# Row sums and sums of squares as accumulated outputs in the first three groups of an adaLN layer (one Trainium2 core)

## The chip, the cores and the metric

The kernel runs on one core of a Trainium2 chip. The time is device microseconds (us) of one execution. Engines: PE is the matrix engine, DVE the vector engine, ACT the scalar engine (activation functions), POOL the GpSimd engine, SP the engine that here only issues loads and stores. Each engine works through its own list of instructions in order; semaphores tie the lists together.

## The reference

One transformer layer on 4 x 1024 tokens of width 256, in float32. A conditioning vector c (one per batch) gives six vectors sa, ca, ga, sb, cb, gb.

```
h   = layernorm(x) * (1 + ca) + sa
q, k, v = unit(h Wq + bq), unit(h Wk + bk), unit(h Wv + bv)     # unit: f = fft; f / (|f| + 1e-8); back
s   = cumsum over tokens of bind(k, v)                          # product of spectra
x   = x + ga * unbind(s, q)                                     # product with the conjugate spectrum
h   = layernorm(x) * (1 + cb) + sb
x   = x + gb * top-2 mixture of 8 experts (swiglu, 256 -> 512 -> 256)
```

layernorm divides by sqrt(variance + 1e-5); the spectra are divided by |f| + 1e-8. These two places are the ones that matter here.

## The kernel before

**Tiles.** The 4096 tokens are 8 groups of 512 (`GT` = 4 tiles of 128 rows); two groups make a batch. A group's x is one tile of 128 x 4 x 256 (`x_tiles[g]`, three buffers), and its result rows are gathered in `row`, 128 x 4 x 266 (two buffers): 256 columns of normalized x, 8 expert weights and 2 numbers. Each group has two pairs of tiles; pairs are numbered 0 to 15 below, pair n belonging to group n // 2.

**Steps of a group.** `begin_group` (L480) takes mean and variance of each of the 512 rows (`moments`, L445: `bn_stats` L451 and `bn_aggr` L453 on DVE), the square root (ACT, L441) and its reciprocal (DVE, L442), and the shift `nmr` (L486, L487); POOL stamps token numbers into `row` (L490).

**Steps of a pair** (`pair`, L496, a generator whose pieces are interleaved with those of other pairs):

- ACT normalizes into `xn` (L505), PE transposes it (L512), ACT copies `ht` (L516);
- PE multiplies by the spectra matrix (L528), ACT copies `z` (L535) and squares it (`sq`, L537 for k and v, L541 for q);
- `magnitudes` (L545): POOL copies two end columns (L547), DVE or POOL adds real and imaginary squares (L551), ACT takes the root (L552), DVE adds EPS (L553). For k and v this is one call over two parts of `mag` (516 columns), then DVE multiplies the two (L556) and takes the reciprocal (L557); for q it is one part (258 columns) and a reciprocal (L562);
- complex products on DVE (L469 to L474, L559) and, for the normalized q, on POOL (L563); the cumulative sum on PE (L569 to L579) with `s` copied by ACT (L587); transposes (L594), `ot` (L598), and the inverse transform (L604);
- DVE adds the result to x (L612), updates the gate (L614), and takes the moments of the new x (L618); root and reciprocal as above; gate and shift (L623, L628); ACT normalizes into `row` (L631), DVE scales and shifts it (L635, L636).

**Routing and experts.** `route` (L639) ranks the 8 gates (L649 to L654, softmax weights on ACT L662, L663), turns them into places (PE L682, L689; `slot_i`, L710), and POOL scatters the 4 tiles twice into the DRAM tensor `slots` (L715, eight indirect DMAs a group). A last step adds the bias part to x (L737, L745) and stores x to `out` (L746). Blocks of 256 slots are then loaded (`x_in`, L865; `w1`, L872), turned (L881), sent through the experts (L918 to L948) and added to `out` by indirect DMA (L962).

**Setup beside it.** While groups 0 and 1 run, `prepare` makes the matrices of the later batches (L338 to L400: PE, ACT copies such as `raw` L374 and L398, DVE L376 to L400), through the PSUM bank `late`, which the routing uses as well.

**Order.** The generators are stepped by the loop at the end of the kernel function. A scheduling layer then orders each engine's list by priorities and inserts the waits; buffers that are used again make the next writer wait for the last reader. The first expert block is begun after group 2 has been routed; the later groups share the engines with expert blocks.

Of the kernel before, what the change touches and what calls it, by code (L numbers as in the profile page):

```python
# [7 lines left out]
FP = mybir.dt.float32  # L8
I32 = mybir.dt.int32
AF = mybir.ActivationFunctionType  # L10
ALU = mybir.AluOpType
AX = mybir.AxisListType

P = 128
D = 256
# [3 lines left out]
GT = 4  # L19
GN = GT * P  # L20
RESERVE = 4
RARE = 2
LATER = 8
PT = 2
# [3 lines left out]
EPS = 1e-8  # L28
# [9 lines left out]
def adaln_layer_kernel(  # L38
# [27 lines left out]
    nc = tc.nc  # L66
# [14 lines left out]
    const = ctx.enter_context(tc.tile_pool(name="const", bufs=1))  # L81
# [10 lines left out]
    def bank(tag, bufs=1):  # L92
        return ps_m.tile([P, 512], FP, tag=tag, name=tag, bufs=bufs)

    def late():
        return bank("late")
# [15 lines left out]
    lower = msk[:, 3 * P :].rearrange("p (e j) -> p e j", j=NE)  # L112
    eps_ln = const.tile([P, 1], FP, name="eps_ln")
    nc.gpsimd.memset(eps_ln, LN_EPS)
    tiny = const.tile([P, 1], FP, name="tiny")
    nc.gpsimd.memset(tiny, 1e-30)

# [50 lines left out]
    two = ctx.enter_context(tc.tile_pool(name="two", bufs=2))  # L168
# [264 lines left out]
        gates_of(b, t)  # L433
        nc.sync.dma_start(out=kept[:, b], in_=t)

    def deviations(mv, tag):

        n = mv.shape[1]
        root = two.tile([P, n], FP, tag=tag + "root", name="root")
        r = two.tile([P, n], FP, tag=tag + "r", name="rstd")  # L440
        nc.scalar.activation(root, mv[:, :, 1], AF.Sqrt, bias=eps_ln)  # L441
        nc.vector.reciprocal(r, root)  # L442
        return root, r

    def moments(src, tag):  # L445

        n = src.shape[1]
        mv = two.tile([P, n, 2], FP, tag=tag + "mv", name="mv")
        st = two.tile([P, n, 6], FP, tag=tag + "st", name="st")
        for i in range(n):  # L450
            nc.vector.bn_stats(st[:, i, :], src[:, i, :])  # L451
        for i in range(n):
            nc.vector.bn_aggr(mv[:, i, :], st[:, i, :])  # L453
        return mv

    def bins(t):

# [22 lines left out]
    def begin_group(g):  # L480

        x4 = x_tiles[g]
        mv = moments(x4, "a")
        root, r = deviations(mv, "a")
        nmr = two.tile([P, GT], FP, tag="nmr", name="nmr")
        nc.vector.tensor_mul(nmr, mv[:, :, 0], r)  # L486
        nc.vector.tensor_scalar(nmr, nmr, -1.0, 1.0, ALU.mult, ALU.add)  # L487
        gate = two.tile([P, GT, NE], FP, tag="gate", name="gate")
        row = rows.tile([P, GT, ROW], FP, tag="row", name="row")
        nc.gpsimd.tensor_copy(  # L490
            row[:, :, D + NE :].bitcast(I32),
            numbers[:, g * GT : (g + 1) * GT, :],
        )
        of_group[g] = root, r, nmr, gate, row

    def pair(g, j):  # L496

        b, first = g // GPB, g % GPB == 0
        x4, pb = x_tiles[g], of_batch[b]
        root, r, nmr, gate, row = of_group[g]  # L500
        xp = x4[:, j : j + PT, :]
        xn = two.tile([P, PT, D], FP, tag="xn", name="xn")
        for k in range(PT):
            i = j + k
            nc.scalar.activation(  # L505
                xn[:, k, :], xp[:, k, :], AF.Identity,
                bias=nmr[:, i : i + 1], scale=r[:, i : i + 1],
# [15 lines left out]
        mag = two.tile([P, PT, 3, P + 1], FP, tag="mag", name="mag")  # L523
# [21 lines left out]
        def magnitudes(lo, hi, eng):  # L545
            for n in range(2):
                nc.gpsimd.tensor_copy(  # L547
                    mag[:, :, lo:hi, n * P : n * P + 1],
                    sq[:, :, lo:hi, n * (D - 1) : n * (D - 1) + 1],
                )  # L550
            eng.tensor_add(mag[:, :, lo:hi, 1:P], sq[:, :, lo:hi, 1:P], sq[:, :, lo:hi, P : D - 1])  # L551
            nc.scalar.activation(mag[:, :, lo:hi, :], mag[:, :, lo:hi, :], AF.Sqrt, bias=tiny)  # L552
            nc.vector.tensor_scalar(mag[:, :, lo:hi, :], mag[:, :, lo:hi, :], EPS, None, ALU.add)  # L553

        magnitudes(1, 3, nc.vector)
        nc.vector.tensor_mul(mag[:, :, 1, :], mag[:, :, 1, :], mag[:, :, 2, :])  # L556
        nc.vector.reciprocal(mag[:, :, 1, :], mag[:, :, 1, :])  # L557
        u = complex_product(k_, v, False)
        nc.vector.tensor_mul(bins(u), bins(u), sliding(mag[:, :, 1, :], 0))  # L559
        yield  # L560
        magnitudes(0, 1, nc.gpsimd)
        nc.vector.reciprocal(mag[:, :, 0, :], mag[:, :, 0, :])  # L562
        nc.gpsimd.tensor_mul(bins(q), bins(q), sliding(mag[:, :, 0, :], 0))  # L563
# [35 lines left out]
        yield  # L599

        po = bank("mid"), late()
        for k in range(PT):
            for h in range(2):
                nc.tensor.matmul(  # L604
                    po[k][:, :IC],
                    lhsT=ot[:, h, k * P : (k + 1) * P],
                    rhs=pb[:, INV + h * IC : INV + (h + 1) * IC],
                    start=(h == 0),
                    stop=(h == 1),
                )  # L610
        for k in range(PT):
            nc.vector.tensor_add(xp[:, k, :], po[k][:, :D], xp[:, k, :])  # L612

            nc.vector.scalar_tensor_tensor(  # L614
                gate[:, j + k, :], z[:, k, 3 * D :], root[:, j + k : j + k + 1],
                po[k][:, D:IC], ALU.mult, ALU.add,
            )
        mv2 = moments(xp, "b")  # L618
        _, r2 = deviations(mv2, "b")
        yield  # L620

        for k in range(PT):
# [2 lines left out]
                ALU.mult, ALU.add,  # L625
            )
        nmr2 = two.tile([P, PT], FP, tag="nmr2", name="nmr2")
        nc.vector.scalar_tensor_tensor(nmr2, mv2[:, :, 0], -1.0, r2, ALU.mult, ALU.mult)  # L628
        h_row = row[:, j : j + PT, :D]
        for k in range(PT):  # L630
            nc.scalar.activation(  # L631
                h_row[:, k, :], xp[:, k, :], AF.Identity,
                bias=nmr2[:, k : k + 1], scale=r2[:, k : k + 1],
# [218 lines left out]
    class Block:  # L852
# [24 lines left out]
        def turn(self):  # L877
# [31 lines left out]
            self.h = mtwo.tile([P, NF // P, BLK], FP, tag="h", name="h")  # L909

        def hidden(self, pair):
            ps = []
            for s in range(2):
# [130 lines left out]
    for t in range(NG * PER + STEPS - HALFWAY + 3):  # L1044
        if t < NG * PER and t % PER == 0:
            g = t // PER
            if 0 < g < NG - 1:
                load_x(g + 1)
            if g % GPB == 1 and g // GPB + 1 in range(2, BATCH):
                load_batch(g // GPB + 1)  # L1050
            begin_group(g)
# [8 lines left out]
        if t < NG * PER and t % HALFWAY == 0:  # L1060
            n = t // HALFWAY
            new = pair(n // PAIRS, n % PAIRS * PT)
            pairs.append([n, 1, new])
            next(new)
        for r in list(routes):
            g, step = r[0], r[1]
            next(r[2])
            r[1] += 1
            if step == 2:
# [4 lines left out]
                if count:  # L1074
# [7 lines left out]
                    left = 3 * (len(queue) + (current[0] is not None))  # L1082
                    rate = max(0, left - RESERVE) / PER
            if step == 3:
# [14 lines left out]

    rare = queue[-RARE:]  # L1100
    del queue[-RARE:]
    usual = len(final_blocks) - RARE
    needed = nc.values_load(
# [77 lines left out]
```

## Time and profile before

| | |
|---|---|
| median of 6 runs | 805.78 us (801.79 to 808.21) |
| profiled execution, its own time | 807.36 us |
| its span | 805.4 us |
| mean granted clock of PE | 0.914 |
| busy: PE, DVE, ACT, POOL | 691.6, 561.0, 326.8, 391.3 us |
| L451 `bn_stats` x64, L453 `bn_aggr` x64 | 24.3, 8.2 us |
| L553 EPS addition, 516 and 258 columns, x16 each | 8.4, 6.1 us |

A profile shows one execution. In the lines of groups a row reads: line of the kernel, engine, operation, output<-input, shape, count, then busy time and mean duration of one, then the idle time just before such instructions and what ended it. In the lines in order of time a row begins with its start and its length; the bracket at its end gives the idle time before it and what ended that. Neighbouring instructions of DVE or ACT overlap by some 0.08 to 0.1 us, so that the spacing of two is a little less than the length of one.

### The profile page before, as it was taken

What the parts mean: (1) busy time and instruction counts of PE and PEld (TensorE: products, weight loads), DVE (VectorE), ACT (ScalarE), POOL (GpSimd) and SP (SyncE); (2) the same over time, 40 slices, a digit from 0 to 9 for tenths busy, and PEclk for the clock granted to TensorE, in tenths of its full rate; (3) what the DMA queues carried; (4) which work ended last, traced back from release to release, by engine and by line L of the source; (5) the groups of instructions that cost most, each with busy time, mean ns of one, the idle gap of its engine ahead of it and who ended that gap; (6) DMA issues with size and microseconds to landing.
All of it is one profiled execution on the core that took longest, in us unless ns stands there. A gap on an engine that the chain in (4) does not pass through costs nothing. (4 is left out here: it accounts for less than half of the span.)

```text
span 805.4 us, 10038 instructions
## 1 busy us (share of the span) xinstructions
PE 691.6 (86%) x2876; PEld 532.1 (66%) x2876; DVE 561.0 (70%) x1570; ACT 326.8 (41%) x606; POOL 391.3 (49%) x391
## 2 busy tenths in 40 slices
PE   6989796586797889799799897989978999999991
PEld 5655554353475657677587675758766888888881
DVE  3688979869466787878697868776935655655650
ACT  4334336154364536464566363634211333232230
POOL 1013153414355564666567656656754545455432
PEclk9899999585599889999999898989989999999996
DMA  9300042310762158328542761365875655766322
GB/s 315 131 0 1 5 177 71 111 69 27 235 178 63 42 131 284 82 52 215 133 86 57 217 151 26 67 206 151 168 223 169 161 143 155 181 168 168 90 40 26
DMA packets 55553, 100.16 MB, mean 124 GB/s; under 512 B 7165, under 2 KB 40586, under 8 KB 54986
## 3 DMA queue, kind: packets, MB, share of 16 engines
q1 hardware_dynamic: 38218, 72.68, 26.5%
q0 software_dynamic: 17280, 26.83, 19.2%
q8 instruction: 25, 0.41, 0.2%
q14 instruction: 30, 0.25, 0.1%
HBM read 72.80 MB, written 27.99 MB: 125 GB/s over the span
## 5 line engine op out<-in xcount | busy, mean ns | idle before, releaser
L918 PE MATMUL gv<-xt,w 128*128 128x256 f32 x1184 | 279.6, 390 | 14.0 <-DVE gt L930 8.6
L918 PEld LDWEIGHTS gv<-xt,w 128*128 128x128 f32 x1184 | 227.6, 196 | 49.4 <-DVE gt L930 10.4
L962 POOL DMA_INDIRECT out_dram<-gb,token x74 | 120.1, 1622 | 59.2 <-DVE gb L958 42.6
L948 PE MATMUL py<-w_sb,h 128*128 x592 | 136.6, 383 | 1.0 <-DVE gb L958 1.0
L901 POOL DMA_INDIRECT gb<-kept_gb,token x74 | 81.7, 1104 | 109.7 <-DMA out_dram<-gb,token 31.9
L934 ACT ACTIVATE sg<-gt 128x512 f32<-128x512 f32 x74 | 46.6, 630 | 205.6 <-DVE gt L930 174.4
L948 PEld LDWEIGHTS py<-w_sb,h 128*128 128x128 f32 x592 | 112.6, 192 | 17.6 <-DVE gb L958 1.4
L528 PE MATMUL in<-batch,ht 128*128 128x512 f32 (+1 forms) x256 | 99.1, 533 | 5.8 <-ACT ht L516 5.8
L715 POOL DMA_INDIRECT slots<-row,slot_i x64 | 67.0, 1046 | 51.5 <-DVE slot_i L710 24.3
L930 DVE TENSOR_SCALAR gt<-gv,bias 128x256 f32<-128x256 f32 x148 | 65.1, 475 | 24.5 <-PE gv L918 24.5
L528 PEld LDWEIGHTS in<-batch,ht 128*128 128x128 f32 x256 | 49.3, 202 | 44.0 <-issue 31.0
L942 POOL TENSOR_TENSOR h<-vt,sg 128x512 f32<-128x512 f32 x42 | 55.2, 1316 | 42.9 <-DVE vt L941 34.0
L937 ACT ACTIVATE vt<-gv,bias 128x256 f32<-128x256 f32 x148 | 61.6, 464 | 17.2 <-PE gv L918 16.8
L940 DVE TENSOR_SCALAR vt<-vt 128x512 f32<-128x512 f32 x74 | 35.6, 480 | 45.2 <-ACT vt L937 41.7
L547 POOL COPY mag<-sq 128x4 f32<-128x4 f32 (+1 forms) x64 | 21.3, 391 | 80.6 <-ACT sq L537 70.1
L941 DVE TENSOR_TENSOR vt<-vt,gt 128x512 f32<-128x512 f32 x74 | 51.8, 701 | 1.6
L535 ACT COPY z<-in 128x512 f32<-128x512 f32 (+1 forms) x64 | 29.6, 479 | 48.7 <-PE in L528 45.7
L958 DVE SCALAR_TENSOR_TENSOR gb<-py,weight,gb 128x256 f32<-128x256 f32 x74 | 32.7, 476 | 17.9 <-PE py L948 17.4
L563 POOL TENSOR_TENSOR z<-z,mag 128x512 f32<-128x512 f32 x16 | 20.6, 1287 | 46.2 <-DVE mag L562 36.0
L594 PE MATMUL mid<-msk,u 128*128 128x128 f32 x64 | 13.7, 319 | 31.7 <-DVE u L472 23.9
L451 DVE BATCH_NORM_STATS2 st<-x 128x6 f32<-128x256 f32 x64 | 24.3, 413 | 15.8 <-DMA x<-in_x_dram 15.8
L594 PEld LDWEIGHTS mid<-msk,u 128*128 128x128 f32 x64 | 8.7, 158 | 39.7 <-issue 36.5
(213 smaller groups left out, 1029.3 us busy)
## 6 DMA issues: line engine op xcount, KB each, us to landing
w<-in_w1t_dram SPq DMA_DIRECT2D x37, 1024.0 KB, 7.6
x_in<-slots SPq DMA_DIRECT2D x37, 266.0 KB, 5.6
x<-in_x_dram SPq DMA_DIRECT2D x8, 512.0 KB, 4.4
w_sb<-in_w2t_dram SPq DMA_DIRECT2D x1, 4096.0 KB, 15.9
out_dram<-x SPq DMA_DIRECT2D x8, 512.0 KB, 5.0
kept<-of SPq DMA_DIRECT2D x2, 1428.0 KB, 4.9
batch<-kept SPq DMA_DIRECT2D x2, 1428.0 KB
slots<-fill SPq DMA_DIRECT2D x9, 266.0 KB, 5.8
```

The lines of the kernel that those rows point to most:

```text
L528: nc.tensor.matmul(pz, lhsT=ht[:, h, k * P : (k + 1) * P], rhs=pb[:, h * HC + lo : h * HC + hi], start=(h == 0), stop=(h == 1),)
L715: s = nc.gpsimd.indirect_dma_start(out=slots, out_offset=bass.IndirectOffsetOnAxis(ap=slot_i[:, n, i : i + 1], axis=0), in_=row[:, i, :], ...
L901: nc.gpsimd.indirect_dma_start(out=self.gb[:, i, :], out_offset=None, in_=kept_gb, in_offset=bass.IndirectOffsetOnAxis(ap=self.token[:, i, ...
L918: nc.tensor.matmul(pp[:, j, :], lhsT=self.w1[:, h, s, f * P : (f + 1) * P], rhs=self.xt[:, h, :], start=(h == 0), stop=(h == 1),)
L930: nc.vector.tensor_scalar(gt[:, j], ps[0][:, j], self.bias[:, self.k, 0, f : f + 1], LIMIT, ALU.add, ALU.min)
L934: nc.scalar.activation(sg, gt, AF.Sigmoid, scale=ALPHA)
L937: nc.scalar.activation(vt[:, j], ps[1][:, j], AF.Identity, bias=self.bias[:, self.k, 1, f : f + 1])
L940: nc.vector.tensor_scalar(vt, vt, LIMIT + 1.0, 1.0 - LIMIT, ALU.min, ALU.max)
L941: nc.vector.tensor_mul(vt, vt, gt)
L942: self.eng.tensor_mul(self.h[:, 2 * pair : 2 * pair + 2, :], vt, sg)
L948: nc.tensor.matmul(py[:, i, :], lhsT=self.h[:, f, i * P : (i + 1) * P], rhs=w2_sb[:, bass.ds(self.e, 1), f, :].rearrange("p a d -> p (a d) ...
L962: s = nc.gpsimd.indirect_dma_start(out=out, out_offset=bass.IndirectOffsetOnAxis(ap=self.token[:, i, 0:1], axis=0), in_=y[:, i, :], in_off ...
```

## The change

In groups 0 to 2 (`g < EARLY`) the statistics behind the pairs are made another way: DVE's addition of the residual becomes a `scalar_tensor_tensor` with an accumulated output, which holds the row sums (`total`); DVE scales them to minus the mean; ACT then squares x - mean with an accumulated output, which holds the sums of squared deviations (`moments_act`). The squares themselves are not used; they are written to the part of `row` that is filled later. In groups 1 and 2 `begin_group` does the same, the row sums being the accumulated output of a copy on ACT into `row`. In group 0 `begin_group` keeps `bn_stats`. In groups 0 to 2 ACT adds EPS to the magnitudes, in the later ones DVE, but now for the first part `lo` alone; that of v (part 2) gets its EPS inside the multiplication that replaces L556, in all groups. Signs follow: `moments_act` returns minus the mean.

```diff
@@
+EARLY = 3
@@
+    eps_mag = const.tile([P, 1], FP, name="eps_mag")
+    nc.gpsimd.memset(eps_mag, EPS)
@@
-    def deviations(mv, tag):
-
-        n = mv.shape[1]
+    def inverse_root(var, scale, tag):
+
+        n = var.shape[1]
         root = two.tile([P, n], FP, tag=tag + "root", name="root")
         r = two.tile([P, n], FP, tag=tag + "r", name="rstd")
-        nc.scalar.activation(root, mv[:, :, 1], AF.Sqrt, bias=eps_ln)
+        nc.scalar.activation(root, var, AF.Sqrt, bias=eps_ln, scale=scale)
         nc.vector.reciprocal(r, root)
         return root, r
@@
-        return mv
+        return mv[:, :, 0], *inverse_root(mv[:, :, 1], 1.0, tag)
+
+    def moments_act(src, total, junk, tag):
+
+        n = src.shape[1]
+        mv = two.tile([P, n, 2], FP, tag=tag + "mv", name="mv")
+        minus = mv[:, :, 0]
+        nc.vector.tensor_scalar(minus, total, -1.0 / D, None, ALU.mult)
+        for i in range(n):
+            nc.scalar.activation(
+                junk[:, i, :], src[:, i, :], AF.Square,
+                bias=mv[:, i, 0:1], accum_out=mv[:, i, 1:2],
+            )
+        return minus, *inverse_root(mv[:, :, 1], 1.0 / D, tag)
@@ begin_group
-        mv = moments(x4, "a")
-        root, r = deviations(mv, "a")
-        nmr = two.tile([P, GT], FP, tag="nmr", name="nmr")
-        nc.vector.tensor_mul(nmr, mv[:, :, 0], r)
-        nc.vector.tensor_scalar(nmr, nmr, -1.0, 1.0, ALU.mult, ALU.add)
         gate = two.tile([P, GT, NE], FP, tag="gate", name="gate")
         row = rows.tile([P, GT, ROW], FP, tag="row", name="row")
+        if 0 < g < EARLY:
+            total = two.tile([P, GT], FP, tag="atotal", name="total")
+            for i in range(GT):
+                nc.scalar.activation(
+                    row[:, i, :D], x4[:, i, :], AF.Copy, accum_out=total[:, i : i + 1]
+                )
+            mean, root, r = moments_act(x4, total, row[:, :, :D], "a")
+        else:
+            mean, root, r = moments(x4, "a")
+        nmr = two.tile([P, GT], FP, tag="nmr", name="nmr")
+        nc.vector.tensor_mul(nmr, mean, r)
+        nc.vector.tensor_scalar(nmr, nmr, 1.0 if 0 < g < EARLY else -1.0, 1.0, ALU.mult, ALU.add)
@@ pair, magnitudes
-            nc.vector.tensor_scalar(mag[:, :, lo:hi, :], mag[:, :, lo:hi, :], EPS, None, ALU.add)
+            if g < EARLY:
+                nc.scalar.activation(
+                    mag[:, :, lo, :], mag[:, :, lo, :], AF.Identity, bias=eps_mag
+                )
+            else:
+                nc.vector.tensor_scalar(
+                    mag[:, :, lo, :], mag[:, :, lo, :], EPS, None, ALU.add
+                )
 
         magnitudes(1, 3, nc.vector)
-        nc.vector.tensor_mul(mag[:, :, 1, :], mag[:, :, 1, :], mag[:, :, 2, :])
+        nc.vector.scalar_tensor_tensor(
+            mag[:, :, 1, :], mag[:, :, 2, :], EPS, mag[:, :, 1, :], ALU.add, ALU.mult
+        )
@@ pair, after the inverse transform
+        if g < EARLY:
+            total = two.tile([P, PT], FP, tag="btotal", name="total")
@@
-            nc.vector.tensor_add(xp[:, k, :], po[k][:, :D], xp[:, k, :])
+            if g < EARLY:
+                nc.vector.scalar_tensor_tensor(
+                    xp[:, k, :], po[k][:, :D], 1.0, xp[:, k, :], ALU.mult, ALU.add,
+                    accum_out=total[:, k : k + 1],
+                )
+            else:
+                nc.vector.tensor_add(xp[:, k, :], po[k][:, :D], xp[:, k, :])
@@
-        mv2 = moments(xp, "b")
-        _, r2 = deviations(mv2, "b")
+        h_row = row[:, j : j + PT, :D]
+        if g < EARLY:
+            mean, _, r2 = moments_act(xp, total, h_row, "b")
+        else:
+            mean, _, r2 = moments(xp, "b")
         yield
@@
-        nc.vector.scalar_tensor_tensor(nmr2, mv2[:, :, 0], -1.0, r2, ALU.mult, ALU.mult)
-        h_row = row[:, j : j + PT, :D]
+        nc.vector.scalar_tensor_tensor(
+            nmr2, mean, 1.0 if g < EARLY else -1.0, r2, ALU.mult, ALU.mult
+        )
```

## The prediction

> **What bounds the kernel now.** I read the busy tenths in 40 slices first, then busy time by stage, then the instructions of each engine in order of time, and last the queue that issues the loads (SP).
>
> ```profile
> PE   6989796586797889799799897989978999999991
> DVE  3688979869466787878697868776935655655650
> ACT  4334336154364536464566363634211333232230
> PEclk9899999585599889999999898989989999999996
> ```
>
> ```profile
> 50.00:100.00 50.00, 42.20 (x153) 27.83 (x154) 43.66 (x118) 20.20 (x39) 9.55 (x15) 0.97 0.00 1
> 100.00:150.00 50.00, 39.37 (x136) 24.39 (x137) 43.54 (x123) 21.38 (x40) 19.38 (x26) 0.87 0.28 105
> 150.00:200.00 50.00, 33.63 (x95) 18.67 (x94) 40.04 (x137) 22.18 (x42) 18.05 (x25) 0.70 0.23 78
> 214.00:600.00 386.00, 343.46 (x1440) 267.98 (x1441) 286.18 (x809) 185.75 (x329) 233.70 (x220) 0.93 0.52 135
> 600.00:792.00 192.00, 184.39 (x872) 159.88 (x870) 111.34 (x245) 53.54 (x114) 93.15 (x69) 0.99 0.56 142
> 122.00:137.00 15.00, 10.59 (x40) 6.76 (x38) 14.15 (x33) 8.12 (x17) 6.23 (x13) 1.00 0.23 70
> 137.20:150.80 13.60, 9.53 (x24) 5.72 (x25) 12.54 (x44) 5.36 (x9) 3.51 (x4) 0.50 0.05 20
> ```
>
> Columns: stage, its length, busy time of PE, PEld, DVE, ACT and POOL, PE's granted clock, DMA share, GB/s. From 40 to 207 us no expert block has begun and DVE is the fullest engine (about 87% from 50 to 150); from 214 on PE is (89%, then 96%). The seam is the moment at which the rows of group 2 are in `slots`, because SP issues the first `x_in` then:
>
> ```profile
> 206.96 0.40 SPq L865 DMA_DIRECT2D x_in<-slots  x1
> ```
>
> So I ask when that moment comes, and let everything behind it shift with it. On the way to it:
>
> ```profile
> 100.94 1.19 POOL L715 DMA_INDIRECT slots<-row,slot_i  x1 [14.26 <-DVE slot_i L710]
> 110.83 0.97 POOL L715 DMA_INDIRECT slots<-row,slot_i  x1 [0.30 <-issue]
> 111.83 1.23 POOL L563 TENSOR_TENSOR z<-z,mag 128x512 f32<-128x512 f32 x1
> 113.49 0.19 POOL L490 COPY row<-numbers 128x8 int32<-128x8 int32 x1 [0.43 <-DMA slots<-row,slot_i]
> ...
> 157.10 1.25 POOL L563 TENSOR_TENSOR z<-z,mag 128x512 f32<-128x512 f32 x1
> 163.23 0.19 POOL L490 COPY row<-numbers 128x8 int32<-128x8 int32 x1 [4.88 <-DMA slots<-row,slot_i]
> ```
>
> ```profile
> 105.00 1.10 ACT L631 ACTIVATE row<-x,nmr,rstd 128x256 f32<-128x256 f32 x2 [2.47 <-DVE nmr L628]
> 105.99 1.57 ACT L505 ACTIVATE xn<-x,nmr,rstd 128x256 f32<-128x256 f32 x3
> 110.68 0.59 ACT L374 COPY raw<-late 128x512 f32<-128x512 f32 x1 [2.00 <-PE late L366]
> 111.97 0.37 ACT L587 COPY s<-mid 128x256 f32<-128x256 f32 x1 [0.70 <-PE mid L579]
> 121.22 1.06 ACT L537 ACTIVATE sq<-z 128x1024 f32<-128x1024 f32 x1
> ```
>
> ```profile
> 167.61 1.40 DVE L451 BATCH_NORM_STATS2 st<-x 128x6 f32<-128x256 f32 x4 [5.43 <-DMA x<-in_x_dram]
> ```
>
> The reader is to see: POOL's stamp on group 2's `row` (L490) waits until group 0's eight scatters have landed, near 113.4, since `row` has two buffers; ACT meanwhile normalizes group 2 into `xn`, which waits for no `row`; and DVE loses 5.43 us to the load of group 4's x.
>
> **The change, part by part.** Durations are of this one execution (span 805.4, its own time 807.36; the median of six is 805.78, 1.58 below). I use spacings of neighbours on DVE: a `bn_stats` 0.34 us, a `bn_aggr` 0.09, the EPS addition 0.34 (516 columns) and 0.21 (258).
>
> *DVE relief up to group 0's slots (100.65).* Group 2's statistics leave DVE: 4 x 0.34 + 4 x 0.09 = 1.72. Group 1's leave too, but at 17 to 22 us DVE waits anyway: 0. Pairs 0 and 1 each lose 2 x 0.34 + 2 x 0.09 = 0.86 and gain a scaling of the sums (0.09, the spacing of a 128x2 step) and two reads of an accumulator. No row shows such a read; its bounds are 0 and 0.19 (the 128x2 copy L474), and I take 0.08, that copy's spacing: 0.61 saved a pair, 1.22. The EPS additions go for three pairs and half of a fourth, 3 x 0.55 + 0.34 = 1.99; the `scalar_tensor_tensor` that takes L556's place costs what L556 does (L379 against L469 at 512 columns: 0.68 and 0.69). Together 4.93, on an engine busy 53.50 of the 60.65 us from 40 to 100.65. Not all gets through: for pair 1 the new program has only rstd's reciprocal next behind the scaled sums, so DVE waits for two Squares, a copy and a square root on ACT (0.59 + 0.50 + 0.59 + 0.30 and the hand-overs, about 2.7 us). I take 2.0 us earlier; bounds 0 and 4.93.
>
> *The new wait.* In groups 1 and 2 the copies and Squares of `begin_group` write the rows, unused, into `row`. For group 1 the buffer is fresh. For group 2 it is group 0's, so ACT's first copy waits for what L490 waits for: landing near 111.4 (113.4 less the 2.0). In the changed program's order these eight stand directly behind pair 2's rows (L631), in front of `raw` (L374), of `s` (L587) and of `xn`. ACT reaches them near 103 and stands still over 8 us. Then four copies (0.37 each, the row of L587), the scaling (0.2), four Squares that each wait for the one before (4 x 0.6, from L505's 0.59), and eight accumulator reads, bounded by 0 and 0.30 (the 128x2 square root), taken at 0.1 as the spacing of L663 is: 1.5 + 0.2 + 2.4 + 0.8 = 4.9. `raw` is copied at 116.3, not 110.68. Behind it queue DVE (its scaling waits for the sums, then L376 for `raw`) and PE (L391 for `raw`). From `raw` to the Squares of pair 4 takes 10.5 us now; the new order needs about the same, with `xn` in it. So these come at +5.3 where they were to come at -2.0: a loss of 7.3.
>
> PE idles about 9 us there. The row that bears on that: after a wait of 5.25 us at 133.7 PE ran 13.6 us at clock 0.50 (last stage above). Four 512-column matmuls take 1.88 us at full clock, so half clock adds up to 1.7 to L391 and 1.9 to L528; bounds 0 and 3.6, I take 2. The Trainium skill's "TensorE: Matmul & The Clock Gate", section "What's actually happening", says that an idle window of about 3.4 us halves the clock and a busy one restores it; by that the price would be about 1.7, as an estimate. Loss with the clock: 9.3.
>
> *Catching up, 121.22 to 194.28.* DVE is busy 62.31 of these 73.06 us, so 10.75 are idle. Three early pairs leave 0.61 + 0.55 each, a later one 0.14: 3.6. In the new order group 4's statistics stand behind group 2's slots, so the 5.43 us wait for its x is gone from this stretch. Against that, POOL's product for pair 5 (L563, 157.10) now stands behind the stamp that waits until 163.2, and DVE's next product (159.82) waits for it until about 164.7. I take 3.6 + 4.4 of the idle time = 8.0; bounds 3.6 and 14.35.
>
> *ACT's additions of EPS* (two of 258 columns a pair, 0.51 by L552) lie beside DVE's work: ACT is busy 26 of 61 us up to 100.65. If that cover went, 12 x 0.51 = 6 us would. The skill's "ScalarE: Activation LUTs", section "Rules for kernel authors", keeps additions on VectorE; by engine time that would make 12 x (0.51 - 0.29) = 2.6 us of loss.
>
> *Groups 3 to 7*: the EPS addition shrinks from 516 to 258 columns, 10 x 0.14 = 1.4 us of DVE beside a PE that is 89% busy: 0, bounds 0 and -1.4. *Activation tables*: the new order holds as many loads as before, 0.
>
> Sum: -2.0 + 9.3 - 8.0 = -0.7. The profiled execution would read 806.7, the median 805.1.
>
> **Rivals.**
> - *Faster: DVE's work decides.* All the removed work gets through, 4.9 + 3.6, and the stall is absorbed by the idle time: 805.8 - 8.5 = 797.3. For it: 87% on DVE, and ACT 42%. Against it: 9 us in which ACT, DVE and PE would all stand still.
> - *Slower: ACT's wait for `row` is paid.* Its place is group 2's first copy. With reads at 0.30 (+1.6), the whole 3.6 for the clock and no idle time won back: -2.0 + 7.3 + 1.6 + 3.6 - 3.6 = +6.9: 812.7. At these prices it decides (over +4) once less than 2.9 us of idle time is won back. For it: the order of ACT; against it: 10.75 idle us on DVE.
> - *Slower: POOL's product behind the stamp.* If the wait of 159.8 to 164.7 is not where the x load made DVE wait, +4.9 on my sum: 810.0.
>
> **How the numbers follow.** A measurement of this kernel tells about 0.5% (4 us) from no change. My case, the parts cancel: 0.40, between 801.8 and 809.8. The faster rival 0.31, the two slower ones 0.17 and 0.12. The range runs from 797, the faster rival, to 813, the dearer slower one; beyond lie the last 1.4 us of gain and the sum of both slower prices, 2 in 10 together.
>
> **What would show it.** ACT idle 7 to 10 us before group 2's first accumulating copy, ended by DMA `slots<-row`; `raw` then near 116; a granted clock of 0.5 soon after 110; the last scatter of group 0 issued near 109; the first `x_in` between 203 and 211, near 206; from there to the end the same 598 us within 3. Wrong if group 2's copies start without a wait, if an accumulator read costs over 0.3 us, or if the stage from 214 to 600 changes length by itself.

## The result, and the profile after

The changed kernel takes 811.28 us (median of 20 runs, 806.24 to 815.52), the kernel before 803.96 (46 runs). The ratio is 1.0089, 95% interval 1.0069 to 1.0109: slower by 0.9%, where no change was forecast (805.1, range 797 to 813). The profiled execution took 810.94 us with a span of 809.2, that is 3.6 above the one of before; the forecast for it was 806.7. Line numbers are now those of the changed kernel. Ratios leave out executions over 1.5% above the fastest of their kernel; only b_eps_all below had such (5 of 12, among them the profiled one).

The busy tenths in 40 slices (20.2 us each) of the changed kernel:

```profile
PE   6998758776798779899799898989978999999991
...
DVE  3698945948658786878597968776925656655650
ACT  4564435544165635554566363624211332232230
...
PEclk9999988776599889989899998999998999999997
```

The hole that was forecast is there: in slice 6 (101 to 121 us) DVE falls from 9 to 4 and PE to 5. The seam, in the instructions of SP in order of time:

```profile
210.93 0.40 SPq L909 DMA_DIRECT2D x_in<-slots  x1
```

The first `x_in` comes at 210.93 instead of 206.96, 3.97 later; from there to the end of the span it is 598.3 us, before 598.4. So all of this execution's loss lies ahead of the seam. Busy time by stage, each stage 4 us later than those shown of before:

```profile
218.00:604.00 386.00, 345.39 (x1451) 270.52 (x1452) 289.88 (x820) 187.85 (x333) 234.60 (x219) 0.93 0.52 135
604.00:796.00 192.00, 183.98 (x862) 159.00 (x861) 110.37 (x243) 52.76 (x112) 92.94 (x69) 0.98 0.56 141
```

They hold nearly what they held before (PE 343.46 and 184.39). On the way to the seam, POOL's instructions in order of time:

```profile
97.38 1.19 POOL L759 DMA_INDIRECT slots<-row,slot_i  x1 [6.68 <-DVE slot_i L754]
...
109.73 0.19 POOL L513 COPY row<-numbers 128x8 int32<-128x8 int32 x1 [1.64 <-DMA slots<-row,slot_i]
...
151.53 1.02 POOL L759 DMA_INDIRECT slots<-row,slot_i  x1 [4.65 <-DVE slot_i L754]
...
163.72 0.19 POOL L513 COPY row<-numbers 128x8 int32<-128x8 int32 x1 [1.71 <-DMA slots<-row,slot_i]
163.87 1.21 POOL L595 TENSOR_TENSOR z<-z,mag 128x512 f32<-128x512 f32 x1
...
198.66 1.03 POOL L759 DMA_INDIRECT slots<-row,slot_i  x1 [5.30 <-DVE slot_i L754]
```

Group 0's scatters start 3.56 earlier (97.38 for 100.94), group 1's 4.93 later (151.53 for 146.60), group 2's 4.10 later (198.66 for 194.56). The time went between the first and the second. There, ACT's instructions:

```profile
100.32 1.09 ACT L675 ACTIVATE row<-x,nmr,rstd 128x256 f32<-128x256 f32 x2 [0.71 <-DVE nmr L671]
109.76 0.42 ACT L504 ACTIVATE row<-x 128x256 f32<-128x256 f32 x1 [8.35 <-DMA slots<-row,slot_i]
110.08 0.19 ACT L504 ACTIVATION_READ_ACCUMULATOR row<-x 128x1 f32 x1
110.18 0.40 ACT L504 ACTIVATE row<-x 128x256 f32<-128x256 f32 x1
...
113.68 0.56 ACT L377 COPY raw<-late 128x512 f32<-128x512 f32 x1
...
118.12 0.37 ACT L401 COPY of<-late 128x256 f32<-128x256 f32 x1 [3.41 <-PE late L394]
...
120.12 2.07 ACT L528 ACTIVATE xn<-x,nmr,rstd 128x256 f32<-128x256 f32 x4
...
130.93 1.06 ACT L560 ACTIVATE sq<-z 128x1024 f32<-128x1024 f32 x1
```

ACT stands still for 8.35 us ahead of group 2's first accumulating copy, until group 0's scatters have landed. `raw` is copied at 113.68 (before 110.68), pair 4's `xn` at 120.12 (before 105.99), its Squares at 130.93 (before 121.22). And DVE's instructions of the same kernel:

```profile
118.52 0.42 DVE L402 TENSOR_SCALAR of<-late 128x256 f32<-128x256 f32 x1 [1.54 <-ACT of L401]
...
119.46 0.16 DVE L512 TENSOR_SCALAR nmr<-nmr 128x4 f32<-128x4 f32 x1
...
165.12 0.69 DVE L485 TENSOR_TENSOR u<-mid,z 128x512 f32<-128x512 f32 x1 [0.94 <-POOL z L595]
...
167.45 0.07 DVE L722 MEMSET earlier<- 128x8 f32 x1
175.68 0.69 DVE L485 TENSOR_TENSOR u<-z 128x512 f32<-128x512 f32 x1 [8.17 <-ACT z L558]
```

The reader is to see two things here. `xn` waits for `nmr` (L512), which stands on DVE behind the step that waits for ACT's copy of `of`; what it is made from (L511) was there at 116.05. And at 167.5, where DVE waited 5.43 us for group 4's x before, it now waits 8.17 us for `z`.

### The profile page after: what moved, and what is told of

Read it like the earlier page. It is cut to its first block, busy times and chain, and to the rows that moved or that the text cites. A ratio compares the mean times of both kernels' runs of the same rounds, so it can differ in the third digit from the quotient of the medians.

```text
span 809.2 us, 10074 instructions
## 1 busy us (share of the span) xinstructions
PE 694.7 (86%) x2876; PEld 534.5 (66%) x2876; DVE 552.8 (68%) x1538; ACT 345.1 (43%) x674; POOL 391.3 (48%) x392
## 5 line engine op out<-in xcount | busy, mean ns | idle before, releaser
L962 PE MATMUL gv<-xt,w 128*128 128x256 f32 x1184 | 285.8, 395 | 14.8 <-DVE gt L974 9.5
L962 PEld LDWEIGHTS gv<-xt,w 128*128 128x128 f32 x1184 | 230.5, 198 | 52.9 <-DVE gt L974 11.6
L781 PE MATMUL late<-batch,w_t 8*128 8x256 f32 x64 | 23.8, 503 | 14.4 <-DVE x L789 11.4
L485 DVE TENSOR_TENSOR u<-z 128x512 f32<-128x512 f32 x16 | 11.5, 718 | 34.3 <-ACT z L558 34.3
```

What stands on the lines that cost most here:

```text
L962: nc.tensor.matmul(pp[:, j, :], lhsT=self.w1[:, h, s, f * P : (f + 1) * P], rhs=self.xt[:, h, :], start=(h == 0), stop=(h == 1),)
```

## The experiments

The theory after the result: ACT's wait for group 0's scatters (1) makes the loss. Its rival: the way of group 2's statistics through ACT and DVE and back (2), wait or no wait. Both leave open why so little was won back behind it, and where the gain comes from that the wait eats up. The runs stand in four sets, each on one chip, beside the kernel before on the same chip, which took 804.4, 810.5, 810.4 and 809.3 us there. So ratios compare within a set; the first `x_in`, read from one profile each (before: 206.96), across them, but two profiles of one kernel can differ: those of the changed kernel by 0.6 us there and by 1.0 at group 0's first scatter.

| run | what it is | first x_in | ratio, 95% interval |
|---|---|---|---|
| set 1: a_junk | changed, unused rows to a tile of their own | 202.10 | 0.9938 (0.9906 to 0.9970) |
| a_bn_g2 | changed, group 2's statistics on DVE | 202.24 | 0.9944 (0.9914 to 0.9975) |
| a_pairs_eps | changed, without the group part | 201.43 | 0.9950 (0.9925 to 0.9975) |
| b_wait | before, and the wait alone | 211.70 | 1.0055 (1.0020 to 1.0090) |
| set 2: b_eps | before, and the EPS part alone | 201.05 | 0.9879 (0.9848 to 0.9909) |
| b_pairs | before, and the pairs' part alone | 205.38 | 1.0019 (1.0001 to 1.0036) |
| a_cold | changed, two idle matmuls | 208.97 | 0.9985 (0.9962 to 1.0007) |
| a_warm | changed, eleven idle matmuls | 212.58 | 0.9998 (0.9970 to 1.0026) |
| set 3: after_same | the changed kernel | 211.53 | 1.0059 (1.0025 to 1.0093) |
| a_cold_same | as a_cold | 207.89 | 1.0027 (1.0001 to 1.0054) |
| a_warm5 | changed, five idle matmuls | 208.82 | 1.0037 (1.0001 to 1.0073) |
| b_eps_same | as b_eps | 200.86 | 0.9935 (0.9907 to 0.9962) |
| set 4: b_nox | before, without the wait for group 4's x | 204.58 | 1.0015 (0.9995 to 1.0034) |
| b_group | before, and the group part alone | 216.65 | 1.0145 (1.0122 to 1.0168) |
| b_eps_group | EPS and group part, tile of its own | 199.94 | 0.9890 (0.9854 to 0.9926) |
| b_eps_all | before, EPS on ACT in all groups | 204.21 | 1.0021 (0.9989 to 1.0054) |

### The wait taken away, and the wait alone

A tile of their own for the rows that nothing reads (a_junk):

```
+            junk = sp.tile([P, GT, D], FP, tag="junk", name="junk")
...
-                    row[:, i, :D], x4[:, i, :], AF.Copy, accum_out=total[:, i : i + 1]
+                    junk[:, i, :], x4[:, i, :], AF.Copy, accum_out=total[:, i : i + 1]
...
-            mean, root, r = moments_act(x4, total, row[:, :, :D], "a")
+            mean, root, r = moments_act(x4, total, junk, "a")
```

> The changed kernel, but the unused rows that the accumulating copies and Squares of groups 1 and 2 write go to a tile of their own instead of row. Theory 1, the wait for row decides: in the changed kernel ACT stood still 8.35 us (101.4 to 109.8) until group 0's scatters had landed; here group 2's copies start without that wait, the 3.6 us by which group 0's scatters came earlier are kept, and some 1 to 2 us are won behind them: first x_in near 202, ratio to the kernel before 0.994 (0.989 to 0.998). Theory 2, the way of the statistics through ACT and DVE and back decides (copies, scaling, Squares, eight accumulator reads, square root, then nmr on DVE): the copies wait for nothing, yet pair 4's Squares stay near 130 and the ratio at 1.005 or above.

Measured: 0.9938, `x_in` at 202.10. The sign of the change turns. But this run takes away more than the wait: with no buffer to wait for, the scheduling layer places group 2's copies and Squares at 41 to 52 us, so the late way of the statistics is gone with the wait.

Group 2 on DVE (a_bn_g2), and no group on ACT at all (a_pairs_eps):

```
-        if 0 < g < EARLY:
+        if 0 < g < 2:
```

> The changed kernel, but group 2's statistics are taken on DVE with bn_stats as before (group 1's and the pairs' stay accumulated). Theory 1 (the wait for row): no ACT work of group 2 writes row early, so the wait is gone; 1.7 us of DVE work come back ahead of group 0's slots, so the scatters start near 99 instead of 97.4; ratio 0.996 (0.991 to 0.999). Theory 2 (the way of the statistics): the same kernel is fast as well, since that way is gone with it; so 0.996 here with 1.005 for the run with a tile of its own would speak for theory 2, and 0.994 and 0.996 for theory 1. If neither holds and the pairs' accumulations or the EPS additions cost the time: 1.005 or above here.

```
-        if 0 < g < EARLY:
+        if False:
...
-        nc.vector.tensor_scalar(nmr, nmr, 1.0 if 0 < g < EARLY else -1.0, 1.0, ALU.mult, ALU.add)
+        nc.vector.tensor_scalar(nmr, nmr, -1.0, 1.0, ALU.mult, ALU.add)
```

> The changed kernel without its part in begin_group: the statistics of groups 1 and 2 are taken on DVE with bn_stats; the pairs' accumulated sums and Squares and the EPS additions on ACT stay. Theory 1 and theory 2 both put the loss on group 2's part, so the ratio is that of the run before within 0.2%: 0.996 (0.991 to 0.999); group 1's statistics fall at a time where DVE waits anyway. A third theory, that each pair's round trip through ACT (two Squares behind DVE's sum, 3.0 us of idle DVE or ACT per pair) costs the time: 1.004 or above.

Measured: 0.9944 and 0.9950, as a_junk within their intervals. Group 2's part in `row` alone turns a gain of 0.5% into a loss of 0.6 to 0.9% (the loss was measured beside other sets; by the profiles its seam is 8.7 us later than a_bn_g2's). These two take both the wait and the way out, so neither parts theory 1 from theory 2.

The wait alone, in the kernel before (b_wait):

```
         row = rows.tile([P, GT, ROW], FP, tag="row", name="row")
+        if g == 2:
+            for i in range(GT):
+                nc.scalar.copy(row[:, i, :D], x4[:, i, :])
```

> The kernel before, with four plain copies on ACT added in begin_group of group 2 alone, from x4 into row's columns, without accumulated outputs; nothing reads what they write. This is the wait with 1.5 us of ACT work and without the statistics. They wait for group 0's scatters, which land near 113.4, and in the program's order two of pair 4's four normalized rows stand in front of them, two behind, and raw, s and of behind. Theory 1: ACT stands still some 5 us ahead of them, raw is copied near 116 instead of 110.7, pair 4's Squares come 5 to 7 us later and about half of it is won back: ratio 1.004 (1.002 to 1.008). Theory 2: without the statistics' way nothing on DVE hangs on it, and the wait is taken up by idle time: 1.000 to 1.001.

ACT's instructions of b_wait in order of time:

```profile
106.45 1.08 ACT L508 ACTIVATE xn<-x,nmr,rstd 128x256 f32<-128x256 f32 x2
113.82 1.32 ACT L492 COPY row<-x 128x256 f32<-128x256 f32 x4 [6.29 <-DMA slots<-row,slot_i]
...
116.52 0.56 ACT L374 COPY raw<-late 128x512 f32<-128x512 f32 x1
...
126.99 1.06 ACT L540 ACTIVATE sq<-z 128x1024 f32<-128x1024 f32 x1
```

Four copies of 1.32 us in all, off every chain of data, cost 0.55% and put the seam 4.74 us later: what they do is hold ACT for 6.29 us with two of pair 4's rows of `xn`, `raw` and `s` queued behind. Squares come 5.77 later, the seam 4.74; only 1.0 is won back. Theory 1 stands for a part.

The group part alone (b_group; pairs and EPS put back as before):

```
-        if g < EARLY:
+        if False:
             total = two.tile([P, PT], FP, tag="btotal", name="total")
...
-            if g < EARLY:
-                nc.scalar.activation(mag[:, :, lo, :], mag[:, :, lo, :], AF.Identity, bias=eps_mag)
+            nc.vector.tensor_scalar(mag[:, :, lo:hi, :], mag[:, :, lo:hi, :], EPS, None, ALU.add)
```

> The kernel before with the group part alone: statistics of groups 1 and 2 by accumulating copies and Squares on ACT that write into row; pairs and EPS as before. Against the kernel before it has the wait and the longer way of the statistics and 1.7 us less DVE work ahead of group 0's slots. If the parts add up: the changed kernel (1.006 to 1.009) over the run without its group part (0.995) makes 1.011 to 1.014. If the loss needs the earlier scatters and moves with them: 1.005, as the wait alone (1.0055).

ACT's instructions of b_group:

```profile
111.69 0.42 ACT L504 ACTIVATE row<-x 128x256 f32<-128x256 f32 x1 [7.08 <-DMA slots<-row,slot_i]
...
115.13 0.56 ACT L377 COPY raw<-late 128x512 f32<-128x512 f32 x1
...
132.48 1.06 ACT L560 ACTIVATE sq<-z 128x1024 f32<-128x1024 f32 x1
```

1.0145, and the parts add up, at the seam (9.69 later here, 5.53 earlier without the group part, 4.16 together; 3.97 was measured) and roughly in ratios of different chips (1.0145 x 0.9950 = 1.0094). `raw` is even earlier than in b_wait (115.13), yet the Squares come at 132.48, 11.26 later than before: with the statistics behind it, the wait costs about twice what it costs alone. So theory 2 holds for the other part: it is what stands behind the wait, the way of the statistics and the order that comes with it, that makes it dear. (In this profile PE also has a second stretch at half clock, from 122 to 130 us, which b_wait's has not; so the Squares alone would show too much, but the ratios, over five and twelve executions, lie still further apart.) Of these 11.26, 9.69 reach the seam; 1.6 is won back.

### What makes the way long: an order, or the clock?

a_cold puts two matmuls that nothing reads on PE ahead of the two that wait for `raw`; a_warm has eleven, a_warm5 five:

```
+        if b == 3:
+            idle = ps_y.tile([P, HALF, D], FP, tag="y", name="idle")
+            for k in range(2):
+                extra = nc.tensor.matmul(
+                    idle, lhsT=ones, rhs=fwd, start=True, stop=True
+                )
+                tc.add_manual_dep(extra.ins, part.ins.name, SYNC, reason="where PE stands still")
```

> The changed kernel with two matmuls of 512 columns, whose result nothing reads, on PE ahead of the two that wait for raw. They change the order a little there: the product with the mask for s stands behind the two that wait for raw, and on DVE group 2's nmr stands ahead of the step that waits for ACT's copy of `of`. PE still stands still over 4 us before raw and its clock is halved as in the changed kernel. It is the control for the next run. If the order alone made part of the loss (nmr at 119.5 behind that step, xn at 120.1), xn comes 3 to 4 us earlier and the ratio falls to 1.005; if it did not, 1.009 as the changed kernel.

> As the run before, but eleven such matmuls: PE works through the 5.9 us in which it stood still, in nearly the same order (two transposes of xn and one copy stand elsewhere). If PE's half clock behind the wait is a part of the loss: the two matmuls behind raw take 1.9 us instead of 3.8, the stretch from raw to pair 4's Squares is 3 us shorter than in the control, first x_in 2 to 4 us earlier, and the ratio 0.003 to 0.005 below the control's. If the clock falls again at once, in the next pause (116 to 119), or its price lies beside other waits: the same ratio as the control within 0.002.

a_warm missed its aim: a matmul of 512 columns is two passes of 0.43 us, the eleven took 9.6 us and held PE up beyond `raw`; its Squares come 2.0 later than the control's and its seam 3.6. And a_cold's 0.9985 can't be set against the changed kernel's 1.0089, which was measured in another set, beside a kernel before of 803.96 us and not 810.5. Hence, on one chip:

> The changed kernel itself, beside the next three on one chip: the kernel before took 804.4 us on one chip and 810.5 us on another, and the ratios of single parts so far come from both. If the ratios carry from chip to chip: 1.009 (1.006 to 1.012). If they do not, because the chip moves the part behind first x_in and not the seam, anything from 0.998 to 1.012, and the next two runs are then read against this one.

> The changed kernel with two idle matmuls of 512 columns ahead of the two that wait for raw, which puts group 2's nmr on DVE ahead of the step that waits for `of`: seen once, with pair 4's Squares at 127.7 instead of 130.9 and first x_in at 209.0 instead of 210.9. If the place of nmr in DVE's order is a part of the loss: 2 to 4 us below the changed kernel on this chip, ratio lower by 0.002 to 0.005. If what that run showed was the chip: the changed kernel's ratio within 0.002.

> As the run before with five such matmuls. One of 512 columns takes two passes of 0.43 us, so eleven took 9.6 us and held the two that wait for raw back by 3.7 us; five take 4.4 and end at 113.6, before raw. If the half clock behind the wait costs on the way: those two take 1.9 instead of 3.5 us and first x_in comes 1.5 us earlier than in the control, ratio lower by 0.002. If its price lies beside other waits: first x_in and ratio as the control's within 1 us and 0.002.

DVE's instructions of a_cold_same:

```profile
115.38 0.16 DVE L519 TENSOR_SCALAR nmr<-nmr 128x4 f32<-128x4 f32 x1
...
117.75 0.42 DVE L409 TENSOR_SCALAR of<-late 128x256 f32<-128x256 f32 x1 [0.49 <-ACT of L408]
```

With `nmr` ahead of that step, `xn` starts 2.33 us after `raw` instead of 6.44, and in both pairs of profiles the seam is earlier: 208.97 for 210.93, 207.89 for 211.53. Of the second difference 1.79 was there at group 0's scatters already (96.59 for 98.38), ahead of the place where the kernels differ; so some 2 us in both pairs. The ratios, 1.0027 for 1.0059, agree, but their intervals overlap. That these 2 us are the place of `nmr` is not shown. From `raw` to the Squares takes 13.43 and 13.40 us here; the changed kernel took 17.25 in its first profile, with a second stretch at half clock, and 13.96 in its second, without one. So where the clock is alike the new place of `nmr` gains 0.6 us, and in that pair most of the gain at the seam arises later, behind group 1's scatters, where the changed kernel waits for a product of POOL.

Instructions of after_same, of POOL, then of ACT, then of DVE:

```profile
163.40 0.19 POOL L513 COPY row<-numbers 128x8 int32<-128x8 int32 x1 [3.24 <-DMA slots<-row,slot_i]
163.56 1.21 POOL L595 TENSOR_TENSOR z<-z,mag 128x512 f32<-128x512 f32 x1
```

```profile
166.74 1.58 ACT L528 ACTIVATE xn<-x,nmr,rstd 128x256 f32<-128x256 f32 x3 [5.22 <-DVE nmr L512]
```

```profile
164.81 0.69 DVE L485 TENSOR_TENSOR u<-mid,z 128x512 f32<-128x512 f32 x1 [3.62 <-POOL z L595]
...
176.36 0.69 DVE L485 TENSOR_TENSOR u<-z 128x512 f32<-128x512 f32 x1 [9.16 <-ACT z L558]
```

This is the order of the prediction's third rival: POOL's product behind the stamp on `row`, and the stamp behind the landing of group 1's scatters. DVE waits 3.62 us for it, group 3's `nmr` stands behind that product on DVE, and `xn` waits 5.22 us for `nmr`. In the first profile the same wait is 0.94 us, in those of a_cold and a_cold_same there is none; in a_bn_g2 and a_pairs_eps it is 3.86 and 4.03, and the kernels gain all the same. No run parts it from the rest.

The clock: PE's instructions of a_warm5, then of a_cold_same.

```profile
108.11 4.46 PE L395 MATMUL idle<-fwd,ones 128*128 128x512 f32 x10
...
113.44 1.98 PE L401 MATMUL late<-wm,silb 128*128 128x512 f32 x4 [0.88 <-ACT raw L377]
...
120.31 1.88 PE L558 MATMUL in<-batch,ht 128*128 128x512 f32 x2
```

```profile
113.87 3.43 PE L401 MATMUL late<-wm,silb 128*128 128x512 f32 x4 [3.76 <-ACT raw L377]
...
120.65 1.12 PE L558 MATMUL in<-batch,ht 128*128 128x512 f32 x2
```

Five matmuls do keep the clock up behind `raw` (1.98 us for 3.43), but then the half clock comes at 120 (1.88 for 1.12), and the seam is no earlier (208.82 for 207.89, though group 0's scatters began 1.3 us earlier). Since the half clock was moved and not taken away, the run doesn't price it: what the clock costs stays open.

### Was the wait for group 4's x worth anything?

b_nox takes that wait away alone; it leaves out group 4's own mean and deviation:

```
-        mv = moments(x4, "a")
+        mv = moments(x_tiles[3] if g == 4 else x4, "a")
```

> The kernel before, but group 4's statistics are taken from group 3's x, which is there long before, so that DVE does not wait 5.43 us (162.1 to 167.6) for group 4's x. Left out: group 4's own mean and deviation. Theory 1, the forecast's step: that wait stands on the way to group 2's slots, and without it DVE goes on earlier; first x_in 4 us earlier, ratio 0.995 (0.993 to 0.997). Theory 2: behind the wait DVE's next product (170.45) waits for z from ACT, which waits for PE's product at half clock; that chain does not hang on the statistics, and DVE stands still there instead: first x_in within 1.5 us, ratio 0.998 to 1.002.

DVE's instructions of b_nox:

```profile
160.87 0.18 DVE L453 BATCH_NORM_AGGREGATE mv<-st 128x2 f32<-128x6 f32 x1
167.97 0.69 DVE L469 TENSOR_TENSOR u<-z 128x512 f32<-128x512 f32 x1 [6.92 <-ACT z L535]
```

The wait for x is gone, and DVE stands still for 6.92 us all the same, for `z`. The seam is 2.38 earlier than in the profile of before, of which 0.59 was there at group 1's scatters already; and DVE's product with pair 5's `mid`, which stands ahead of the place, comes 2.02 earlier (157.80 for 159.82), so the order moved too; some 0.4 us is left for the wait itself. The time did not fall (1.0015). Theory 2, though the seam moved more than the 1.5 us that it allowed.

### Where the gain is

EPS alone (b_eps, b_eps_same), as in the change, and pairs alone (b_pairs: the change without its EPS and group parts):

```
+            if g < EARLY:
+                nc.scalar.activation(mag[:, :, lo, :], mag[:, :, lo, :], AF.Identity, bias=eps_mag)
...
-        nc.vector.tensor_mul(mag[:, :, 1, :], mag[:, :, 1, :], mag[:, :, 2, :])
+        nc.vector.scalar_tensor_tensor(
+            mag[:, :, 1, :], mag[:, :, 2, :], EPS, mag[:, :, 1, :], ALU.add, ALU.mult
+        )
```

> The kernel before with the change's EPS part alone: ACT adds EPS to the magnitudes of groups 0 to 2, DVE adds it to 258 columns instead of 516 in the later groups, and one addition goes into the product. 2.0 us of DVE work go ahead of group 0's slots. Theory A, DVE's removed work comes through one for one where DVE is 88% busy: group 0's scatters 2 us earlier, first x_in 2 to 4 us earlier, ratio 0.997 (0.994 to 0.999). Theory B, ACT's two additions lie on the way (sqrt, addition, reciprocal) and cost what DVE saves: 1.000 to 1.002.

> The kernel before with the EPS part alone, which gave 0.988 on a chip where the kernel before took 810.5 us. If the EPS part brings all of the gain (first x_in at 201.1, 5.9 us earlier than in the kernel before, as in the run without the group part): 0.993 (0.989 to 0.996) where the kernel before takes 804 us. If the pairs' part has a share in the gain after all: 0.996 or above.

> The kernel before with the pairs' part alone: DVE's addition of the residual accumulates the sum, ACT's Square the squares, for the six pairs of groups 0 to 2. By the rows of the changed kernel (accumulator read on DVE 0.08 us, scaling 0.16, two Squares at 0.5 spacing on ACT) each pair loses 0.6 us on DVE and gains 0.9 us of ACT and one more hand-over. Theory A: DVE's 1.2 us ahead of group 0's slots come through, ratio 0.998 (0.995 to 1.000). Theory B: the hand-over costs more than DVE gains: 1.000 to 1.003. The run without the group part gave 0.995 for both this and EPS; the two ratios' gains should add up to that.

POOL's instructions of b_eps:

```profile
97.30 1.18 POOL L727 DMA_INDIRECT slots<-row,slot_i  x1 [10.86 <-DVE slot_i L722]
...
142.84 1.02 POOL L727 DMA_INDIRECT slots<-row,slot_i  x1 [1.09 <-DVE slot_i L722]
```

The EPS part brings group 0's scatters 3.6 us earlier by itself (97.30 for 100.94; in the second profile 4.6), and the seam 5.9 and 6.1. The pairs' part relieves nothing there: its scatters begin at 101.81, those of three kernels that are as before up to there (before, b_nox, b_wait) between 100.38 and 101.39; and the time doesn't fall (1.0019), though the seam is 1.6 earlier. So all of the relief was the EPS part's.

The remaining two: EPS and group part with a tile of its own for the unused rows as in a_junk (b_eps_group; shown is what goes of the pairs' part), and EPS on ACT in all eight groups (b_eps_all, one line in b_eps).

```
-        if g < EARLY:
+        if False:
             total = two.tile([P, PT], FP, tag="btotal", name="total")
...
-        if g < EARLY:
+        if False:
             mean, _, r2 = moments_act(xp, total, h_row, "b")
```

> The EPS part and the group part with a tile of its own for the unused rows, so without the wait; the pairs' statistics stay bn_stats. If statistics on ACT relieve DVE once the wait is gone: 1.7 us earlier than the EPS part alone at group 0's slots, ratio 0.989 (0.986 to 0.992). If DVE's relief is worth nothing there: 0.993 as the EPS part alone.

```
-EARLY = 3
+EARLY = 8
```

> The EPS part in all eight groups: ACT adds EPS to 258 columns everywhere, DVE nowhere. Up to the first x_in as the EPS part alone (201), after it ACT's ten additions more (5 us) and DVE's 10 x 0.21 us fewer stand beside a PE that is 89 per cent busy: 0.993 as the EPS part alone within 0.002 if they are hidden; 0.996 or above if ACT's copies for PE come later by them.

b_eps_group has the earliest seam of all, 199.94, 0.9 to 1.1 ahead of the EPS part alone, at a ratio of 0.9890: it beats both kernels. It lies between the two ratios of the EPS part alone (0.9879 and 0.9935, other chips), so whether statistics on ACT are worth anything on top is not settled. b_eps_all gives the gain away (1.0021, against 0.988 to 0.9935) with twenty additions more on ACT (two a pair, not the ten that were expected). POOL's instructions of b_eps_all:

```profile
142.83 1.04 POOL L727 DMA_INDIRECT slots<-row,slot_i  x1 [1.09 <-DVE slot_i L722]
...
192.10 1.03 POOL L727 DMA_INDIRECT slots<-row,slot_i  x1 [1.09 <-DVE slot_i L722]
```

Group 1's scatters begin as in b_eps (142.84), group 2's 3.28 us later (188.82 there), and the seam is 3.16 later: so in this profile, of an execution of 819.91 us, a part of the loss lies in group 3, ahead of the seam, and not where PE is the fullest engine. POOL's product (L575) moved ahead of group 2's scatters there, so additions and order aren't parted, and what is lost behind the seam can't be read from one such execution. That is the other side of a rule in the Trainium skill's "ScalarE: Activation LUTs", "Rules for kernel authors", which gives additions to VectorE: it didn't hold in groups 0 to 2, where DVE was 88% busy, and the two ratios agree with it for the groups behind them.

## Why the prediction was wrong, point by point

**What bounds the kernel** was right for the profile shown: all shifts with the seam, and 598 us follow it to 0.1 us; in the second profile it is 600.6.

**The new wait** was right in kind, place and size. Forecast: ACT idle 7 to 10 us, ended by the landing of `slots<-row`; measured 8.35. Copies, scaling, Squares and reads were put at 4.9 us up to `raw`; 3.9 (109.76 to 113.68). A read of the accumulator is an instruction of its own, 0.19 us long at a spacing of 0.10 on ACT, as taken. The last scatter of group 0 was forecast near 109; 107.12. `raw` was forecast at 116.3 and came at 113.68, since the relief was larger and that stretch shorter. The first `x_in` lies at 210.93 in a window of 203 to 211, at its far end, and at 211.53 in the second profile, outside it.

**From raw to the Squares**, "about the same" 10.5 us as before, failed: 17.25 in the profile (13.96 in the second one). In the sum of the prediction this step was treated as unchanged, though `xn` had moved from ahead of `raw` to behind it. From the second profile to a_cold_same, with `nmr` placed earlier, it falls by 0.6 us; the 3.3 between the two profiles go with the second stretch at half clock. (The sum also slipped: 116.3 and 10.5 make 126.8, which is +5.6 and not +5.3.)

**The half clock**, put at 2 of 3.6 us, was there. Two executions of the same changed kernel, by windows of busy time (columns as before; the clock is the third figure from the end), first the one shown above, then after_same:

```profile
113.00:118.00 5.00, 3.70 (x4) 1.17 (x4) 2.70 (x7) 1.70 (x7) 0.00 (x0) 0.50 0.00 0
121.00:128.00 7.00, 7.00 (x17) 3.79 (x16) 1.68 (x4) 2.37 (x5) 0.00 (x0) 0.54 0.71 284
```

```profile
113.00:118.00 5.00, 2.64 (x3) 1.17 (x4) 2.66 (x7) 2.76 (x11) 0.00 (x0) 0.50 0.00 0
121.00:128.00 7.00, 6.94 (x25) 3.95 (x26) 2.73 (x7) 3.78 (x8) 0.00 (x0) 1.00 0.72 284
```

One has a second stretch at half clock and the other has not; the Squares come 9.71 and 7.48 us later than before, the seam 3.97 and 4.57. So what the second stretch took was not left at the seam; but the two profiles also differ in the wait for POOL's product, 0.94 and 3.62, and the first stretch is in both, so the clock's price isn't shown. The Trainium skill's "TensorE: Matmul & The Clock Gate", section "What's actually happening", says that the window by which the clock is decided runs freely, so that the same program meets it at other places; these two executions agree.

**Relief up to group 0's slots**, 2.0 us: 3.56 in the profile, 2.56 in the second. The split was wrong: the EPS additions, 1.99 us of removed work, gave 3.6 to 4.6, more than they took; the pairs' statistics, booked as 1.22 saved, gave nothing. Why the EPS part gives more than its own work was not tried.

**Catching up**, 8.0 us, is the step that failed in both profiles. Measured, from the Squares of pair 4 to the seam: 9.71 - 3.97 = 5.7, and 7.48 - 4.57 = 2.9 in the second profile. Its two terms apart: b_wait and b_group, which have the stall and none of the removed work behind it, win back 1.0 and 1.6, where 4.4 was booked for idle time; the rest, 4.1 to 4.7 in one profile and 1.3 to 1.9 in the other, is left for the removed work, booked at 3.6. That idle time was read from DVE's 5.43 us wait for group 4's x; b_nox shows that it was no reserve, because a wait for `z` stood beside it. After group 1's scatters little is won back: +4.93 becomes +3.97, and in the second profile, with the wait for POOL's product, +3.00 becomes +4.57.

**The sum**, by the same steps: -3.56 + 13.27 - 5.74 = +3.97, and in the second profile -2.56 + 10.04 - 2.91 = +4.57, where -2.0 + 9.3 - 8.0 = -0.7 was forecast. So the stall with its way to the Squares was put 4.0 and 0.7 us too low and catching up 2.3 and 5.1 too high; the larger relief gave back 1.6 and 0.6.

**The rivals.** "ACT's wait for `row` is paid" (+6.9, 812.7) is what came in kind: it was to decide once less than 2.9 us of idle time is won back, and 1.0 to 1.6 is. That its +6.9 lies near the ratio's 7.2 us is luck: the seam moved by 4.0 and 4.6, and the reads that it priced at 0.30 us took 0.10. The rival with POOL's product behind the stamp, put at +4.9, came in part: the product stood there (163.87 behind 163.72), and DVE's next product came at 165.12 and 164.81, where about 164.7 was forecast; it waited 0.94 us for it in the first profile and 3.62 in the second. The faster rival is what the change does without the group part in `row` (seam -5.5, ratio 0.9950). **ACT's additions of EPS** cost less in three groups than they saved on DVE (b_eps).

Open: the two profiles put the seam 4.0 and 4.6 us later, the ratios 1.0089 and 1.0059 make 7.2 and 4.8 us. What lies behind the seam is 593 to 605 us long in the profiles of these kernels (613.9 in b_eps_all's), one execution each, so that the rest can't be placed. In sets 1 and 3 the change of the time is that of the seam within 1.5 us; in set 2 and for b_nox the two differ by 3 to 6 us, and in all of these but b_eps in sign too.

## What to carry to other kernels

Give the unused output of an accumulating instruction a place of its own: a convenient buffer brings its readers' wait with it, and behind it the whole queue of the engine. Idle time of an engine is a reserve only if its next instruction waits for nothing else; read what that instruction would wait for next before any of it is booked as won back. And test the parts of a change alone: here one part gave the gain, one gave nothing, and one took it away and more.

## What the runs showed of the hardware that was not expected

- The same program took 804.4 us on one chip and 809.3 to 810.5 us on three others (medians of 23 to 35 runs), and the EPS part's ratio was 0.9879 and 0.9935 on two of them.
- Keeping PE busy through a pause moved the half clock instead of avoiding it: with five idle matmuls it came at 120.6 instead of 113.4, after pauses of only 0.88 and 1.60 us. With eleven there was none from 104 to 135, but they held PE up by 3.7 us.
- DVE's read of the accumulator took 0.08 us and delayed its next instruction by nothing: the one behind it started at the same time, 96.66.
